# Matrix units and the constant part given other rows in each quarter of an involution and ternary convolution block

## The chip, the core and the metric

The kernel runs on one core of a Trainium2 chip. The metric is the device time of one execution in microseconds (us). The kernel before takes 2158.66 us, the median of 3 runs (2156.32 to 2168.02).

On the core, five engines run side by side, each in the order of its own instructions: TensorE (PE in the profile, its weight loads PEld), VectorE (DVE), ScalarE (ACT), GpSimd (POOL) and SyncE (SP), which issues most of the DMAs. An instruction waits on semaphores for what it needs from other engines.

## What is computed

The input `x` is 8 images of 256 channels, 56 x 56 pixels. Two layers follow each other. The first is an involution: at every pixel and for each of 16 groups of 16 channels a 7 x 7 kernel is made from the normalized input (256 to 64 to 16 x 49 numbers), and the pixel's surroundings are summed with it. The second normalizes, and runs two 3 x 3 convolutions with weights quantized to -1, 0 and 1, each with a batch norm.

```python
# layer 0
ker = einsum('bchw,oc->bohw', gn(x), w_reduce) + b_reduce
ker = (einsum('bchw,oc->bohw', ker, w_span) + b_span).reshape(B, 16, 1, 49, H, W)
patches = ...                                # 7x7 surroundings of gn(x), 16 groups of 16 channels
x = x + (ker * patches).sum(axis=3).reshape(B, C, H, W)
# layer 1
y1 = relu(batch_norm(tri_conv(gn(x), w1)))
x = x + relu(y1 + batch_norm(tri_conv(y1, w2)))
```

`gn` is a group norm of 32 groups. Its scale and shift in layer 0 are not applied to the data: the scale goes into weights and into the outgoing scaling, and the shift times the sum of a pixel's kernel is a "constant part" that is added by itself.

## The kernel before

**Phases.** A first phase does the involution for all images and stores the result, `x1`, to DRAM. Beside it, VectorE finds the quantizing thresholds of the two convolution weights and quantizes them in pieces, a piece at a time (`quantize`, lines 283 to 334; its VectorE work comes four rows apart, in two steps). Then come the two convolutions (`conv_phase`), and a last elementwise pass. The change concerns the first phase only.

**Quarters and rows.** An image is worked off in four quarters `c` of 64 channels (4 groups each). Both halves of the image's height lie side by side on the 128 partitions. A quarter is worked off in ten rows `ty`; rows 0 to 8 stand for three rows of pixels, row 9 for one. `r = c * 10 + ty` counts an image's 40 rows. The main loop (from line 986) goes through the 32 quarters, and in each through the ten rows.

**What a row does**, in the order of the text:

- `store_x1` of the last quarter (rows 2 and 3) or `load_x` of the next image (some rows): DMAs on SP.
- `apply_row` (line 852): TensorE multiplies the pixels' surroundings `q` with the kernel matrices `a` into a PSUM tile `pa` (two of them).
- `prefetch`: the DMA of a `q` for a row five rows ahead, on SP.
- steps of `norm`, which makes the next image's parameters from row 20 on; statistics of the next image and of the finished rows (`gn1_stats`, `gn2_stats`), on VectorE. In row 1, `gn2_stats` takes the last rows of the quarter before.
- `pick_out`: ScalarE (line 862) and VectorE (864) scale the right group of `pa` into `inv`, and GpSimd (868) adds it to `x`.
- `surround`: GpSimd fills the rim of a loaded `q`, three rows ahead (line 751), ScalarE its lower end in two rows of a quarter (764). `rim_of` in row 1 makes the fills for the next quarter (739, 742).
- some steps of `gen`, as many as a table says: this is what the change touches.
- in some rows, a strip: `reduce` makes a part of the next image's 64 reduced features `kr` (TensorE 713, ScalarE 722). Nine strips make an image's features.
- a step of `quant`, the quantizing of the convolution weights, on VectorE.

**The generator.** `generate` makes the next quarter's matrices in 14 units. `UNITS` lists them as (pair of groups, first column, number of columns): six units of 3, 3, 2, 3, 3 and 2 columns, which also have a narrow edge part (`rest`), then eight of 4 columns. Each unit takes a pair of PSUM banks (there are three pairs, `ps_p`, shared with strips and the constant part), TensorE fills it (line 820), ScalarE takes one group out of it (824) and VectorE the other (828). After the units come the two steps of `constant`: TensorE (786) multiplies the features with sums of weights, ScalarE applies the shift (794), and GpSimd adds it to the next quarter's `x` (800), in four operations for the two steps. So a quarter has 16 steps in all, and what is left over is run after row 9.

`PER_ROW` says how many steps of `gen` each row takes; it is one list for every quarter:

```python
PER_ROW = (2, 2, 2, 1, 2, 2, 1, 2, 2, 0)
```

The units are thus at 2, 2, 2, 1, 2, 2, 1, 2 in rows 0 to 7, and the two steps of the constant part in row 8. Below, u0 to u13 are a quarter's units in their order.

**The order.** `pin` ties each engine's instructions to the order of the text, row by row, so what stands above is the order on every engine.

Of the kernel before, what the change touches and what calls it, by code (L numbers as in the profile page):

```python
# [52 lines left out]
         for gp in range(GP) for p0, n in part]  # L53


STRIPS = {24: (0, 0, 3), 26: (0, 3, 3), 27: (0, 6, 4),
          28: (1, 0, 3), 29: (1, 3, 3), 31: (1, 6, 3),
          32: (2, 0, 3), 33: (2, 3, 3), 34: (2, 6, 3)}
A_COLS = (NT * NP + NE * PX) * GQ

PER_ROW = (2, 2, 2, 1, 2, 2, 1, 2, 2, 0)
NQB = 5
PLEAD = 2
RIM_AT = 1
# [25 lines left out]
def involution_tri_block_kernel(  # L90
# [488 lines left out]
    with ExitStack() as ph1:  # L579
# [25 lines left out]
        def load_x(b, c, j):  # L605

            if j == 0:
                xs[b, c] = xpool.tile([P, NHW], F32, tag="x", name=f"x_{b}_{c}")
            part = slice(j * NHW // 2, (j + 1) * NHW // 2)
            nc.sync.dma_start(xs[b, c][:, part], x[b, c, :, part])  # L610
# [47 lines left out]
        def gn2_params(b0, b1):  # L658

            yield from group_norm_params(  # L660
                mv2[:, b0:b1].rearrange("p b t s -> p (b t) s"),
                gn2h[:, b0:b1].rearrange("p b t s -> p (b t) s"), ps_one, f"gn2_{b0}")

            for h in range(2):
                rows = slice(h * CH, (h + 1) * CH)
                nc.vector.tensor_copy(gn2[rows, b0:b1], gn2h[rows, b0:b1, h::2, :])
# [38 lines left out]
        def reduce(b, py, i0, m):  # L705

            ps = ps_pair(f"pk_{b}_{py}_{i0}")
            r0 = i0 * PY + py
            for c in range(NCQ):
                for h in range(2):  # L710
                    rows = slice(h * CH, (h + 1) * CH)
                    src = xs[b, c].rearrange("p (r w) -> p r w", w=W)
                    nc.tensor.matmul(ps[h][:, :m * W], wrn[rows, c, :],  # L713
                                     src[rows, r0:r0 + (m - 1) * PY + 1:PY, :],
                                     start=(c == 0), stop=(c == NCQ - 1))
            whole = min(m, TY - 1 - i0)
            for h in range(2):
                src = ps[h][:, :m * W].rearrange("p (k x) -> p x k", x=PX)
                for n0, k0, k1 in ((h * NT // 2 + i0 * TX, 0, whole * TX),
                                   (NT + h * TX, whole * TX, m * TX)):  # L720
                    if k0 < k1:
                        nc.scalar.activation(kr[py][:, :, n0:n0 + k1 - k0], src[:, :, k0:k1],
                                             AF.Identity, bias=brn)
# [79 lines left out]
        def generate(b, c, a):  # L803

            whole, rest = (v.rearrange("q t (g p) -> q g p t", g=GQ) for v in views(a))
            for u, (gp, p0, n) in enumerate(UNITS):
                ps = ps_pair(f"pg_{b}_{c}_{u}")
                nt = NT + (NE if p0 < PX else 0)  # L810
                g = 2 * gp
                parts = [(whole, 0, NT)] + ([(rest, NT, nt)] if NT < nt else [])

                for j in range(n):
                    py, px = (p0 + j) // PX, (p0 + j) % PX
                    o = py * QX + px
                    for i in range(2):
                        rows = slice(i * CR, (i + 1) * CR)
                        dst = ps[0][:NQ, j:n * nt:n] if i == 0 else ps[1][:NQ, j * nt:(j + 1) * nt]
                        nc.tensor.matmul(dst, wl[rows, c, gp, o:o + NQ], kr[py][rows, px, :],  # L820
                                         start=True, stop=True)
                for j in range(n):
                    for dst, t0, t1 in parts:
                        nc.scalar.activation(  # L824
                            dst[:, g + 1, p0 + j], ps[1][:NQ, j * nt + t0:j * nt + t1],
                            AF.Identity, bias=bt[:, c, g + 1, p0 + j:p0 + j + 1])
                for dst, t0, t1 in parts:
                    nc.vector.tensor_tensor(  # L828
                        dst[:, g, p0:p0 + n].rearrange("q p t -> q t p"),
                        ps[0][:NQ, t0 * n:t1 * n].rearrange("q (t p) -> q t p", p=n),  # L830
                        bt[:, c, g, p0:p0 + n].unsqueeze(1).to_broadcast([NQ, t1 - t0, n]), ALU.add)
                yield
            yield from constant(b, c)

        def apply_row(b, c, a, ty):


            ps = ps_a.tile([P, 512], F32, tag="pa", name=f"pa_{b}_{c}_{ty}")
            row_ps[:] = [ps]
            q = loads.pop((b, c, ty))  # L840
            whole, rest = views(a)
            if ty < TY - 1:
                av, n, t0, t1 = whole, NP, ty * TX, (TY - 1 + ty) * TX
            else:
                av, n, t0, t1 = rest, PX, 0, TX
            m = 32 if ty < TY - 1 else CH
            w = n * m * GQ // CH
            for k in range(TX):
                for h, t in enumerate((t0, t1)):
                    for g in range(CH // m):  # L850
                        o = h * CH + g * m
                        nc.tensor.matmul(ps[o:o + m, k * w:(k + 1) * w], q[:NQ, k, o:o + m],  # L852
                                         av[:, t + k, g * w:(g + 1) * w], start=True, stop=True)
            return ps, n, w // n
# [19 lines left out]
        def prefetch():  # L874
            if queue:
                k = queue.pop(0)
                loads[k] = load_q(*k)
                bare.append(k)
# [9 lines left out]
        def store_x1(b, c, h):  # L888
            nc.sync.dma_start(
                x1_d[b][c // 2][c % 2 * CH:(c % 2 + 1) * CH, h * NHW:(h + 1) * NHW],  # L890
                xs[b, c][h * CH:(h + 1) * CH])
# [3 lines left out]
        def gn2_stats(b, c, ty):  # L895

            if ty == 1:
                gst[b, c] = (small.tile([P, NCB, 6], F32, tag="gn_st2", name=f"st2_{b}_{c}"), 0)
            st, j = gst[b, c]
            while j < NCB and ((j + 1) * NC <= ty * PY * W or ty == TY):  # L900
                image_stats(st, xs[b, c], j)
                j += 1
            gst[b, c] = (st, j)
            if ty == TY:
                nc.vector.bn_aggr(mv2[:, b, c, :], st.rearrange("p n s -> p (n s)"))
# [25 lines left out]
        def matrices(m):  # L931
            return (apool if m % 2 == 0 else apool1).tile(
                [P, A_COLS], F32, tag=f"a{m % 2}", name=f"a_{m}")
# [22 lines left out]

        for i, strip in enumerate(STRIPS.values()):
            reduce(0, *strip)
# [27 lines left out]
        for m, (b, c) in enumerate(quarters):  # L986
            a = a_next
            gen = iter(())
            if m + 1 < len(quarters):
                a_next = matrices(m + 1)  # L990
                gen = generate(*quarters[m + 1], a_next)
            more = b + 1 < B
            for ty in range(TY):
                r = c * TY + ty

                if last is not None and ty in (2, 3):
                    store_x1(*last, ty - 2)
                elif more and r in X_AT:
                    load_x(b + 1, X_AT.index(r) // 2, X_AT.index(r) % 2)
                row = apply_row(b, c, a, ty)  # L1000
                prefetch()

                if r == PARAMS_AT:
                    norm = params(b + 1) if more else gn2_params(0, b)
                next(norm, None)

                if ty == 1 and last is not None:
                    gn2_stats(*last, TY)
                elif ty >= 2:
                    gn2_stats(b, c, ty - 1)  # L1010
                if more and 4 <= r < 20:
                    gn1_stats(b + 1, (r - 4) // NCB, (r - 4) % NCB)
                pick_out(b, c, ty, *row)
                surround()
                if ty == RIM_AT and m + 1 < len(quarters):
                    rim_of(*quarters[m + 1])
                next(norm, None)
                for _ in range(PER_ROW[ty]):
                    next(gen, None)
                if more and r in STRIPS:  # L1020
                    reduce(b + 1, *STRIPS[r])
                if m * TY + ty >= QUANT_AT:
                    next(quant, None)
                pin()
            for _ in gen:
                pass
            last = b, c
# [162 lines left out]
```

## Time and profile before

| what | value |
|---|---|
| median of 3 runs | 2158.66 us |
| profiled execution | 2164.76 us |
| its span, first to last instruction | 2163.0 us |
| mean granted TensorE clock | 0.911 |
| first phase's rows, first apply to last | 62 to 1049 us |
| kernel matrices on TensorE (line 820) | 6144 matmuls, 466.1 us |
| apply on TensorE (line 852) | 17024 matmuls, 290.4 us |
| matrices taken out by ScalarE (824), by VectorE (828) | 530.1 us, 280.9 us |
| constant's adds on GpSimd (800) | 127.2 us, 1024 ns each |
| fill of the rims on GpSimd (751, largest form) | 225.5 us, 705 ns each |

In the lists, a line names a source line, an engine and an operation with what it writes and reads; then come the number of executions, busy time, and the mean of one. A wait `A <- B` is idle time of A that ended when B was done; "issue" is idle time that no semaphore of the profile explains. Durations of neighbours overlap, since engines begin an instruction before the one ahead of it has left. The profiled execution's time is 1.8 us above its span.

### The profile page before, as it was taken

How to read it: one execution, taken by the hardware profiler on the slowest of the kernel's cores; microseconds unless marked ns; L12 is line 12 of the kernel's file. 1: busy time of each engine (PE TensorE's matmuls, PEld its weight loads, DVE VectorE, ACT ScalarE, POOL GpSimd, SP SyncE). 2: the span in 40 equal slices, each digit the busy share in tenths (PEclk: the TensorE clock that was granted, in tenths of full speed). 3: DMA queues.
4: the chain of work that ended last, by engine and by line, in shares of the span. 5: the costliest groups of instructions: out<-in, count | busy, mean ns of one | idle time of the engine just before them, and what ended most of it. 6: DMA issues, size and time to landing. Idle time of an engine off the chain costs nothing.

```text
span 2163.0 us, 70724 instructions
## 1 busy us (share of the span) xinstructions
PE 1759.3 (81%) x29680; PEld 1632.6 (75%) x29680; DVE 1753.4 (81%) x3337; ACT 1432.2 (66%) x3553; POOL 590.7 (27%) x965
## 2 busy tenths in 40 slices
PE   4988988989899898988699999997999999960000
PEld 4777777878777687777699999997999999960000
DVE  5777978787777868877699999998999999984444
ACT  3877787877767677777366666665566666653344
POOL 0555566555546646666200000000000000000000
PEclk9999999999989999999799999998999999985555
DMA  5667777686767758667733333335323333369999
GB/s 184 212 178 232 220 211 236 195 266 197 244 185 218 239 164 263 191 203 201 254 122 122 122 122 122 122 122 189 118 114 124 124 128 128 124 262 425 429 428 397
DMA packets 156250, 440.06 MB, mean 203 GB/s; under 512 B 63774, under 2 KB 74012, under 8 KB 148508
## 3 DMA queue, kind: packets, MB, share of 16 engines
q1 hardware_dynamic: 150336, 405.50, 55.2%
q10 hardware_dynamic: 5596, 30.03, 3.3%
q8 instruction: 235, 3.85, 0.8%
q14 instruction: 83, 0.68, 0.1%
HBM read 323.28 MB, written 112.20 MB: 201 GB/s over the span
## 4 chain that ended last, share of the span: by engine, by line
PE 68%; DMA 10%; DVE 9%; issue 6%; POOL 3%; ACT 3%; ACTq 0%; SPq 0%; POOLq 0%; DVEq 0%
PE c L522 40%; PE pg L820 14%; PE pa L852 8%; PE pk L713 3%; DMA y1f<-y1d 3%; DMA x1f<-x1d 2%; PE ks L786 2%; DMA out_y<-x1f 2%; POOL q L751 1%; DVE x1f L1102 1%; DVE inv L864 1%; ACT a L824 1%; DMA y2f<-y2d 1%; POOL x L868 1%; DMA q<-in_x_nb 1%
## 5 line engine op out<-in xcount | busy, mean ns | idle before, releaser
L522 PE MATMUL c<-pl,wq 128*128 128x392 f32 x4608 | 857.7, 348 | 14.9 <-ACT pl L392 14.9
L522 PEld LDWEIGHTS c<-pl,wq 128*128 128x128 f32 x4608 | 855.7, 190 | 16.7 <-ACT pl L392 15.3
L824 ACT ACTIVATE a<-pg,bt 126x126 f32<-126x126 f32 (+1 forms) x2048 | 530.1, 469 | 110.1 <-PE pg L820 109.5
L820 PE MATMUL pg<-kr,wl 64*126 64x140 f32 (+1 forms) x6144 | 466.1, 296 | 41.2 <-issue 16.4
L820 PEld LDWEIGHTS pg<-kr,wl 64*126 64x126 f32 x6144 | 405.5, 198 | 67.2 <-issue 24.3
L852 PE MATMUL pa<-a,q 126*32 126x48 f32 x17024 | 290.4, 215 | 67.0 <-issue 52.6
L852 PEld LDWEIGHTS pa<-a,q 126*32 126x32 f32 x17024 | 242.1, 116 | 135.4 <-issue 83.6
L828 DVE TENSOR_TENSOR a<-pg,bt 126x504 f32<-126x504 f32 (+4 forms) x640 | 280.9, 480 | 54.4 <-PE pg L820 52.8
L868 POOL TENSOR_TENSOR x<-x,inv 128x168 f32<-128x168 f32 x320 | 167.0, 522 | 404.1 <-DVE inv L864 370.7
L864 DVE SCALAR_TENSOR_TENSOR inv<-pa,gn1s,inv 128x168 f32<-128x168 f32 (+1 forms) x384 | 134.2, 351 | 154.6 <-ACT inv L862 151.1
L392 ACT CAST pl<-r 128x812 fp32r<-128x812 f32 x192 | 162.5, 868 | 143.4 <-DVE r L387 122.8
L372 POOL MEMSET xp<- 128x116 f32 x32 | 6.3, 196 | 826.1 <-DVE a L387 826.1
L751 POOL TENSOR_TENSOR q<-q,sides 126x256 f32<-126x256 f32 (+1 forms) x320 | 225.5, 705 | 3.1 <-DMA q<-in_x_nb 3.1
L393 DVE TENSOR_TENSOR pl<-r,pl 128x812 fp32r<-128x812 f32 x192 | 186.6, 998 | 27.6 <-ACT pl L392 26.3
L457 ACT ACTIVATE dummy<-y,nc 128x1568 f32<-128x1568 f32 (+1 forms) x128 | 200.2, 1564 | 4.8 <-DVE y L542 3.5
L862 ACT ACTIVATE inv<-pa,gn1s 128x168 f32<-128x168 f32 x320 | 134.9, 423 | 69.5 <-PE pa L852 49.3
L149 DVE BATCH_NORM_STATS2 st<-x 128x6 f32<-128x392 f32 x256 | 137.8, 554 | 16.4 <-DMA x<-in_x 10.1
L800 POOL TENSOR_TENSOR x<-x,add 128x504 f32<-128x504 f32 (+1 forms) x128 | 127.2, 1024 | 25.4 <-ACT add L794 25.4
L1049 ACT ACTIVATE xp<-raw,gn 128x392 f32<-128x392 f32 (+1 forms) x124 | 82.5, 721 | 61.3 <-DVE a L387 61.0
L1069 ACT ACTIVATE xp<-raw,bi_bn,sc_bn 128x392 f32<-128x392 f32 (+1 forms) x124 | 82.3, 720 | 58.8 <-DVE a L387 57.1
L1100 DVE SCALAR_TENSOR_TENSOR y1f<-y2f,sc_bn,y1f 128x3136 f32<-128x3136 f32 (+2 forms) x20 | 56.6, 2831 | 64.6 <-DMA y2f<-y2d 50.6
L713 PE MATMUL pk<-x,wrn 64*128 64x168 f32 (+1 forms) x1152 | 101.0, 316 | 0.0
(174 smaller groups left out, 1789.2 us busy)
## 6 DMA issues: line engine op xcount, KB each, us to landing
q<-in_x_nb SPq DMA_DIRECT2D x320, 448.0 KB, 4.2
raw<-x1d SPq DMA_DIRECT2D x32, 812.0 KB, 5.9
raw<-y1d SPq DMA_DIRECT2D x32, 812.0 KB, 6.1
x<-in_x SPq DMA_DIRECT2D x64, 392.0 KB, 5.3
x1d<-x SPq DMA_DIRECT2D x64, 392.0 KB, 5.2
y1d<-y SPq DMA_DIRECT2D x30, 784.0 KB, 3.7
y2d<-y SPq DMA_DIRECT2D x30, 784.0 KB, 3.4
y1f<-y1d SPq DMA_DIRECT2D x14, 1568.0 KB, 14.4
```

Source lines behind the costliest of these rows:

```text
L392: nc.scalar.copy(hi, r)
L393: nc.vector.tensor_tensor(lo, r, hi.bitcast(F32), ALU.subtract)
L457: nc.scalar.activation(dst, v, f, bias=shift[:, to:to + 1], accum_out=stats[:, to, j, n:n + 1])
L522: nc.tensor.matmul(ps[:, to, :NM], wq[k][:, t, dx, to * P:(to + 1) * P], part[:, t, :, dx:dx + W], start=(c == 0), stop=(c == last))
L713: nc.tensor.matmul(ps[h][:, :m * W], wrn[rows, c, :], src[rows, r0:r0 + (m - 1) * PY + 1:PY, :], start=(c == 0), stop=(c == NCQ - 1))
L751: nc.gpsimd.tensor_tensor(v, v, z, ALU.add)
L820: nc.tensor.matmul(dst, wl[rows, c, gp, o:o + NQ], kr[py][rows, px, :], start=True, stop=True)
L824: nc.scalar.activation(dst[:, g + 1, p0 + j], ps[1][:NQ, j * nt + t0:j * nt + t1], AF.Identity, bias=bt[:, c, g + 1, p0 + j:p0 + j + 1])
L828: nc.vector.tensor_tensor(dst[:, g, p0:p0 + n].rearrange("q p t -> q t p"), ps[0][:NQ, t0 * n:t1 * n].rearrange("q (t p) -> q t p", p=n), ...
L852: nc.tensor.matmul(ps[o:o + m, k * w:(k + 1) * w], q[:NQ, k, o:o + m], av[:, t + k, g * w:(g + 1) * w], start=True, stop=True)
L864: nc.vector.scalar_tensor_tensor(iv, parts[:, :, g], scale[:, g:g + 1], iv, ALU.mult, ALU.add)
L868: nc.gpsimd.tensor_tensor(xv, xv, iv.rearrange("p t (y x) -> p y t x", x=PX), ALU.add)
```

## The change

The list of steps becomes a list for each of the four quarters, and the first strip goes from row 24 to row 25.

```diff
-STRIPS = {24: (0, 0, 3), 26: (0, 3, 3), 27: (0, 6, 4),
+STRIPS = {25: (0, 0, 3), 26: (0, 3, 3), 27: (0, 6, 4),
           28: (1, 0, 3), 29: (1, 3, 3), 31: (1, 6, 3),
           32: (2, 0, 3), 33: (2, 3, 3), 34: (2, 6, 3)}
...
-PER_ROW = (2, 2, 2, 1, 2, 2, 1, 2, 2, 0)
+PER_ROW = ((2, 2, 1, 2, 1, 2, 1, 2, 1, 2), (2, 2, 1, 2, 1, 2, 1, 2, 1, 2),
+           (2, 2, 2, 2, 2, 1, 1, 1, 1, 2), (2, 1, 1, 1, 1, 2, 2, 2, 2, 2))
...
-                for _ in range(PER_ROW[ty]):
+                for _ in range(PER_ROW[c][ty]):
                     next(gen, None)
                 if more and r in STRIPS:
                     reduce(b + 1, *STRIPS[r])
```

Each new list adds up to 16 as well. The strips are in rows 5 to 9 of quarter 2 (before: 4, 6, 7, 8, 9) and in rows 1 to 4 of quarter 3. A row with a strip takes one unit, but for row 9 of quarter 2, which has a strip and the constant part. In quarters 0 and 1 the rows take two units and one by turns from row 1 on. The constant part's two steps come in row 9 of each quarter.

## The prediction

> **What bounds the kernel now.** I read the page first (engine shares, slices, the chain of waits), then the windows of one image by quarter, then the list of waits, then the timeline around one quarter boundary.
>
> ```profile
> span 2163.0 us, 70724 instructions
> PE 1759.3 (81%) x29680; PEld 1632.6 (75%) x29680; DVE 1753.4 (81%) x3337; ACT 1432.2 (66%) x3553; POOL 590.7 (27%) x965
> PE   4988988989899898988699999997999999960000
> POOL 0555566555546646666200000000000000000000
> PE c L522 40%; PE pg L820 14%; PE pa L852 8%; PE pk L713 3%; DMA y1f<-y1d 3%; DMA x1f<-x1d 2%; PE ks L786 2%; DMA out_y<-x1f 2%; POOL q L751 1%; DVE x1f L1102 1%; DVE inv L864 1%; ACT a L824 1%; DMA y2f<-y2d 1%; POOL x L868 1%; DMA q<-in_x_nb 1%
> ```
>
> POOL is busy in the first 20 slices of 54 us only: that is the first phase, 62 us (first apply of a row) to 1049 us, and the only one that the change touches. The convolutions after it and the final pass stay. In the first phase PE is at 8 to 9 tenths, and all four engines are well loaded. The windows of the fourth image, one line per quarter (columns: length, then busy PE, PEld, DVE, ACT, POOL, granted clock, DMA share):
>
> ```profile
> 430.87:461.78 30.91, 23.29 (x744) 19.61 (x741) 26.29 (x69) 23.28 (x83) 17.02 (x29) 1.00 0.83 275
> 461.78:490.42 28.64, 24.94 (x741) 21.18 (x741) 25.31 (x69) 21.46 (x78) 19.30 (x31) 0.94 0.80 238
> 490.42:527.61 37.19, 34.90 (x852) 30.25 (x849) 26.05 (x74) 26.96 (x95) 21.45 (x33) 0.91 0.55 178
> 527.61:555.99 28.38, 27.41 (x806) 23.76 (x804) 19.58 (x47) 24.46 (x88) 15.33 (x28) 1.00 0.69 213
> ```
>
> The reader is to see two kinds of quarters. In the fourth (strips in rows 1 to 4) PE is busy 27.4 of 28.4 us: no order of units can give much. In the first two PE idles, 7.6 and 3.7 us, and DVE is busier than PE. I took the start of every apply row from the timeline: over the first seven images the quarters last 30, 29, 38 and 28 us, while the shortest execution of each row, added up, gives 21.8, 22.7, 31.8 and 26.6. So some 22 us an image are lost, nearly all in quarters 0, 1 and rows 0 to 4 of quarter 2. What ends PE's waits from 60 to 1050 us (columns: us in total, times, longest):
>
> ```profile
> PE pa L852 <- issue: 52.6, 49, 3.2
> ACT sq_a L137 <- DVE ve_a L135: 17.3, 7, 4.0
> PE pg L820 <- issue: 16.4, 11, 4.3
> PE pg L820 <- ACT a L824: 13.2, 12, 2.4
> PE pg L820 <- DVE a L828: 10.4, 10, 2.0
> PE pa L852 <- POOL q L751: 9.4, 6, 5.1
> ```
>
> The largest, "issue", about 69 us, ends no semaphore: it falls in the middle of an apply row too, and counted along PE's stream nearly all such stalls over 0.3 us begin multiples of 256 instructions apart. The clock drops to half in 23 stretches, 137 us together, nearly each behind a gap of 1 to 3 us, so a gap costs more than itself.
>
> The boundary before the fourth image, POOL, DVE and PE lines:
>
> ```profile
> 430.95 4.00 POOL L800 TENSOR_TENSOR x<-x,add 128x504 f32<-128x504 f32 x4
> 434.91 0.30 POOL L868 TENSOR_TENSOR x<-x,inv 128x56 f32<-128x56 f32 x1
> 435.18 0.72 POOL L751 TENSOR_TENSOR q<-q,sides 126x256 f32<-126x256 f32 x1
> 433.47 1.29 DVE L317 TENSOR_TENSOR piece_w<-piece_w 128x48 f32<-128x48 f32 x1
> 434.68 0.34 DVE L318 TENSOR_TENSOR piece_w<-piece_w 128x48 f32<-128x48 f32 x1
> 436.97 0.60 PE L820 MATMUL pg<-kr,wl 64*126 64x140 f32 x5 [1.61 <-DVE a L828]
> ```
>
> The constant's adds hold POOL for 4.00 us. The last row's own add and the fill of the next quarter's row 2 stand behind them, the weight pieces on DVE are stretched by them (0.20 us elsewhere for the L317 form), and PE waits 1.61 us for the unit that DVE gets to late.
>
> **What the Trainium skill says.** "SBUF — State Buffer", § "SBUF: two separate sides": DVE and GpSimd share one port pair as an exclusive lock, held for a whole instruction, against DVE operations with two SBUF inputs. The trace agrees: 1.29 us instead of 0.20. "TensorE: Matmul & The Clock Gate", Part 1: the clock goes to half after an idle window of about 3.4 us. The trace shows half clock in multiples of 3.4 us, but behind shorter gaps (1.5 to 2.5 us). "Runtime: NRT & Kernel Launch", § "Instruction fetch mechanics": instructions come in blocks of 256 by a DMA queue of the sequencer's own, mostly hidden. The stalls at multiples of 256 fit the block, not the word "hidden".
>
> **The change part by part.** No instruction is added or removed: every quarter still runs 14 units and 2 constant steps, every image 9 strips. The moved steps issue no DMA, so SP's queue keeps its order; they pass other work on PE, ScalarE, DVE and POOL alone. PE's work is unchanged, about 103 us an image by the shortest rows; only waits and slow clock can move.
>
> *Constant from row 8 to row 9.* Before, rows 8 and 9 take 2.59 and 0.94 us at full clock; with a unit (0.92) in row 8 and the constant's matmuls (2.59 - 0.85 for a lone apply = 1.7) in row 9 they take about 1.8 and 2.6. POOL's adds still begin about when row 0 of the next quarter begins (430.95 against 430.87 here; they follow the constant's ScalarE adds, which start within a microsecond of its matmuls). But POOL now has, ahead of them, row 9's add (0.30) and the fill for row 2 (0.72); behind them row 0's add (0.54) and the fill for row 3 (0.73). Old slack: adds end at +2.8 to +4.0, the fill at +3.9 to +5.0, row 2 due at +2.36 + 2.12 = 4.5. New: the fill at +5.1 to +6.3, row 3 due at 4.5 + 1.6 = 6.1 (row 2 has one unit in quarters 0 and 1). That is some 0.4 us better. PE's waits for the fill at a row 2 were 0.86, 1.64, 0.70 and 0.62: 3.8 us; I take 3 us off.
>
> *Weight pieces of a row 9.* They follow row 9's picking on DVE. Row 9 is longer by 1.7 us and the adds begin at its end instead of its start, so the five operations run in about 1 us instead of the 3 here. That should remove the PE waits on DVE of 1.90 (189 us), 1.61 (437) and 2.00 (721), 5.5 us, and two stretches of half clock of 3.4 us, worth 1.7 each. I take 7 off these 8.9. The last rows' statistics in row 1, which waited 0.89 us on DVE behind row 9's add at 591, also come free: under 1 us.
>
> *Quarter 2.* In images 0 to 2 the parameter matmul at row 2.0 waits 1.3 to 2.5 us for DVE's statistics, which the longer row 9 would shorten. It gains nothing: the square root on ScalarE, which waits for DVE's chain up to 4.03 us, holds units up next. Rows 0 to 4 took 21.3, 22.1 and 19.5 us in the images with the wait, and 20.8, 23.3, 23.1, 20.3 in those without. I take zero. Rows 0 to 2 are as before (2, 2, 2), row 3 gets a second unit while ScalarE is still late (two units and a pick, 2.5 us, against PE's 3.3 with the parameter matmuls), row 4 loses its strip. Cover: three pairs of PSUM banks, two units of lead. Cost 0 to 0.5 us an image, taken 1 us in all. Rows 5 to 9 have ScalarE at 13 us against PE's 16, so no wait; they already ran without gaps.
>
> *Quarter 3* is PE-bound before and after: zero. *Strips:* only the first moves, row 24 to 25, away from the parameters' last step: zero to 0.3 us an image, taken as zero.
>
> *Quarters 0 and 1, single units spread.* ScalarE's unit costs 1.3 us for three columns with the edge, 1.03 for four, 0.88 for two (from runs of 12, 8 and 10 operations), PE's 0.75, 0.92, 0.50. Rows 0 to 2 want 3.0 + 2.6 + 2.6 of ScalarE against 6.6 of PE; with u5 moved to row 3 the peak of its lag falls by some 0.3 us. On the other side the constant's two pairs are now taken right ahead of row 0, where the third is all that is free: 0 to 0.7 us per boundary, taken 1.5 us in all, the rest being the rival below. Strips and pieces that follow row 0 and 1 meet the adds as before: plus 1.
>
> *Fetch.* The shortest stretches of 128 matmul pairs by the row times: 20% under 3.3 us before, 18% after. Taken as zero, with 5 us either way.
>
> Sum: -3 - 7 - 0.5 + 1 + 1.5 + 1 = about -7 us. The profiled execution took 2164.8 us (span 2163.0), so about 2157.5 under the profiler; against the median shown, 2158.7, this is 2151.5. I say 2151.
>
> **Rivals.** *Cascade:* the waits feed each other, through the half clock and through ScalarE behind DVE. Half of the named dependency waits of PE (13.2 + 10.4 + 9.4 of the list, and 5.3 at row 2.0: 38) would go, 19 us, and with them some 9 us of slow stretches: 2131. For it: 137 us at half clock follow such gaps. Against: half of these sit behind fetch stalls or the square root. *Slower:* the constant's two PSUM pairs. At row 0, the second unit may start only when ScalarE has drained the first constant pair, about 1.3 us after it is filled if ScalarE is on time; PE reaches that unit 2.45 us after. If ScalarE is more than 1.1 us late at row 9 this binds, in a place where the old order had an empty row; behind the waiting matmul stand all of PE's later rows, and the reading of these by ScalarE and DVE. At 0.7 us each over 31 boundaries: +22 us, 2181. For it: ScalarE needs about 22 us a quarter, as PE does. *Reshuffle:* the loss is set by fetch and square root, and nothing moves: 2157.
>
> **How the numbers follow.** Forecast (0 to -15 us) 0.46; cascade 0.21; slower 0.21; reshuffle 0.12. 0.5% is 10.8 us, about what a measurement here can tell from no change. A third of the forecast's chance and nearly all the cascade's lie beyond it: faster 0.37. Slower 0.20, the same 0.43. Range: down to the cascade's middle, up to most of the slower case, 2132 to 2174; the forecast's own is 2144 to 2159.
>
> **What would show it.** Right: POOL's 0.30 add of row 9 and the next fill stand ahead of the four adds; pieces' operations after row 9 near 0.2 us; PE's waits on DVE under 6 us and on the fill under 7; the square root's 17 us and the issue's 69 as before. Wrong: new PE waits on ScalarE in rows 0 and 1 (slower), or a total of half clock under 110 us (cascade).

## The result and the profile after

| | before | after |
|---|---|---|
| median of 20 runs each, us | 2161.54 | 2163.97 |
| profiled execution, us | 2164.76 | 2159.04 |
| its span, us | 2163.0 | 2157.3 |
| mean granted TensorE clock | 0.911 | 0.917 |

The ratio of the times is 1.0005, with a 95% interval of 0.9988 to 1.0021. The change makes no difference that can be told. The forecast of -7 us would be 0.9968 and lies outside the interval.

The two profiled executions differ by 5.7 us in the change's favour, but they are a lucky pair: the one before lies 3 us above its kernel's median, the one after 5 us below its own, and the 20 runs of the changed kernel spread from 2152.7 to 2173.1 us. Their clocks mislead in the same way. Over the 136 executions of the kernel before that ran beside the experiments below the mean granted clock was 0.9154, and over the 20 of the changed kernel 0.9146. So one execution can't decide a question of 7 us. In what follows the traces tell where waits went, and repeated runs tell what that was worth.

The page of the kernel after:

```profile
span 2157.3 us, 70705 instructions
PE 1748.1 (81%) x29680; PEld 1619.6 (75%) x29680; DVE 1751.9 (81%) x3337; ACT 1436.7 (67%) x3553; POOL 588.1 (27%) x965
```

The busy time of every engine is the same within 13 us. The first phase, from its first apply row to the end of its last, takes 982.2 us, and took 985.6; the rest is the same within 2.3 us. The fourth image by quarter (columns: length, then busy PE, PEld, DVE, ACT, POOL, granted clock, DMA share, GB/s):

```profile
434.13:465.29 31.16, 23.15 (x743) 19.56 (x741) 25.33 (x69) 21.93 (x82) 18.01 (x29) 1.00 0.83 268
465.29:493.75 28.46, 24.52 (x743) 20.93 (x741) 25.57 (x68) 22.09 (x82) 18.27 (x30) 0.94 0.83 247
493.75:531.62 37.87, 34.53 (x851) 29.98 (x849) 26.09 (x71) 28.05 (x96) 19.80 (x32) 0.91 0.57 177
531.62:560.90 29.28, 27.61 (x806) 23.72 (x804) 20.26 (x49) 23.99 (x90) 16.45 (x28) 1.00 0.66 206
```

No quarter is more than 1 us away from its length before, and PE still idles 8.0 and 3.9 us in the first two. But the reasons of the idling are others. What ends waits from 60 to 1050 us (us in total, times, longest):

```profile
PE pa L853 <- issue: 70.4, 66, 3.0
...
ACT sq_a L138 <- DVE ve_a L136: 18.3, 7, 3.3
...
PE pg L821 <- issue: 13.2, 12, 3.0
PE pg L821 <- ACT a L825: 12.1, 12, 1.8
...
PE pa L169 <- DVE d_a L166: 10.9, 7, 2.6
...
PE pa L853 <- POOL q L752: 6.1, 2, 5.7
...
PE pg L821 <- DVE a L829: 1.9, 3, 1.0
```

(The lines of the source are one further on than before.) The wait for a unit's VectorE part fell from 10.4 to 1.9 us, the wait for a fill from 9.4 to 6.1, all of it at the phase's end. Two grew: "issue" from 69.0 to 83.6, and one that was 1.2 us before, a matmul of the parameters (L169) that waits for VectorE's square of differences (L166), to 10.9. All of PE's gaps in the phase's rows, added up along the trace, were 117.2 us and are 123.4. The time at half clock was 136.5 and is 109.2 us, but by the clocks of the many runs above that difference belongs to these two executions and not to the change.

The boundary before the fourth image, lines of POOL, DVE and PE, to be read beside the boundary in the prediction. Row 0 begins at 434.13:

```profile
434.25 0.32 POOL L869 TENSOR_TENSOR x<-x,inv 128x56 f32<-128x56 f32 x1 [2.62 <-PE ks L787]
434.53 0.72 POOL L752 TENSOR_TENSOR q<-q,sides 126x256 f32<-126x256 f32 x1
435.21 3.95 POOL L801 TENSOR_TENSOR x<-x,add 128x504 f32<-128x504 f32 x4
434.20 0.20 DVE L318 TENSOR_TENSOR piece_w<-piece_w 128x48 f32<-128x48 f32 x1
...
435.24 1.29 DVE L321 SCALAR_TENSOR_TENSOR piece_w<-piece_w 128x48 f32<-128x48 f32 x1
...
437.23 1.46 PE L821 MATMUL pg<-kr,wl 64*126 64x140 f32 x20
```

Row 9's own add and the next fill now stand ahead of the four adds of the constant part, three of the five weight operations run at 0.2 to 0.3 us (the fourth takes 0.76, and the last, beside the adds, 1.29), and PE goes on with row 1's units with no wait for VectorE. That is the order that the prediction described. The adds, however, begin 1.1 us after row 0 (before: 0.1), because row 9's add, ahead of them on POOL, waits for VectorE's picking of row 9, and that comes at 433.3 to 434.2. At the boundary ahead of quarter 2, counted from its row 0 and averaged over the eight images, the adds began at +0.62 and ended at +4.59 us, and now begin at +1.52 and end at +5.45.

Row 2.1 of the second image shows what these late adds meet (POOL, DVE, PE lines of the kernel after):

```profile
246.03 3.92 POOL L801 TENSOR_TENSOR x<-x,add 128x504 f32<-128x504 f32 x4
...
247.77 0.75 DVE L165 TENSOR_TENSOR d_a<-mv,gm_a 128x4 f32<-128x4 f32 x1
248.55 1.17 DVE L166 TENSOR_TENSOR d_a<-d_a 128x4 f32<-128x4 f32 x1
...
249.77 0.39 PE L169 MATMUL pa<-d_a,grp_sb 128*128 128x4 f32 x2 [2.61 <-DVE d_a L166]
```

Two operations on four elements a partition take 0.75 and 1.17 us beside the adds, and PE stands 2.61 us for the second of them, with row 2.1's units behind it. The square itself was stretched before, too (columns: shortest, median and longest, in ns):

```profile
L165 DVE TENSOR_TENSOR d_a<-d_a x7: 403/1178/1187, 121.5 to 875.4; 128x4 f32<-128x4 f32 x7
```

In the first three images it took 0.40 us, since the wait for the statistics at row 2.0 held the chain until the adds were over; in the other four it took 1.18. Now that this wait is gone, the chain meets the adds in all seven images, and its first operation is stretched as well (a median of 0.21 us before, 0.89 after). One wait has thus taken the other's place: rows 0 and 1 of quarter 2 together take a mean of 7.5 us before and after.

The other new loss is "issue". Such a stall in the middle of an apply row, PE's lines of the kernel after:

```profile
191.20 0.80 PE L853 MATMUL pa<-a,q 126*32 126x48 f32 x55
194.94 0.24 PE L853 MATMUL pa<-a,q 126*32 126x48 f32 x1 [2.95 <-issue]
```

A row's 56 matmuls stop after 55 for 2.95 us, with nothing that the last of them waits for. The DMA part of the page has a queue for PE's instructions:

```profile
q8 instruction: 235, 3.85, 0.7%
```

It moved 235 packets, 3.85 MB: 16 KB each, one for 256 PE instructions. The stall above ends 1.5 us after such a packet, which was on its way from 192.53 to 193.43 us. Of the issue stalls over 1 us, 28 of 29 before and 31 of 35 after end 1.2 to 1.65 us after the end of one. In the first phase a packet sets out a median of 1.5 us after PE has passed the block boundary before it (0.2 to 3.5 for nine in ten), so PE has about one block in hand: 101 of 193 blocks before and 100 after are entered within 1.7 us of their landing. In the convolutions the packets land 22 to 29 us ahead, which is also about one block, since they follow each other there by about 24 us. "Runtime: NRT & Kernel Launch", § "Instruction fetch mechanics", of the Trainium skill has the block of 256 right; its "mostly hidden" doesn't hold for this phase, with 69 and 84 us of stalls.

### The profile page after: what moved, and what is told of

Same layout as the page of the kernel before. It is cut to its first block, busy times and chain, and to the rows that moved or that the text cites. A ratio compares the mean times of both kernels' runs of the same rounds, so it can differ in the third digit from the quotient of the medians.

```text
span 2157.3 us, 70705 instructions
## 1 busy us (share of the span) xinstructions
PE 1748.1 (81%) x29680; PEld 1619.6 (75%) x29680; DVE 1751.9 (81%) x3337; ACT 1436.7 (67%) x3553; POOL 588.1 (27%) x965
## 3 DMA queue, kind: packets, MB, share of 16 engines
q8 instruction: 235, 3.85, 0.7%
## 4 chain that ended last, share of the span: by engine, by line
PE 69%; DMA 10%; issue 7%; DVE 6%; POOL 5%; ACT 3%; SPq 0%; ACTq 0%; POOLq 0%; DVEq 0%
PE c L523 40%; PE pg L821 15%; PE pa L853 9%; DMA x1f<-x1d 4%; PE pk L714 3%; DMA y1f<-y1d 3%; POOL q L752 2%; DMA out_y<-x1f 2%; POOL x L869 2%; PE ks L787 1%; ACT a L825 1%; DVE x1f L1103 1%; POOL x L801 1%; DVE a L829 1%; DMA sums<-in_w_all 1%
## 5 line engine op out<-in xcount | busy, mean ns | idle before, releaser
L825 ACT ACTIVATE a<-pg,bt 126x126 f32<-126x126 f32 (+1 forms) x2048 | 537.4, 474 | 95.5 <-PE pg L821 94.0
L821 PE MATMUL pg<-kr,wl 64*126 64x140 f32 (+1 forms) x6144 | 464.8, 295 | 27.7 <-issue 13.2
L863 ACT ACTIVATE inv<-pa,gn1s 128x168 f32<-128x168 f32 x320 | 135.5, 424 | 72.7 <-PE pa L853 53.8
L150 DVE BATCH_NORM_STATS2 st<-x 128x6 f32<-128x392 f32 x256 | 137.8, 554 | 10.4 <-DMA x<-in_x 9.4
L801 POOL TENSOR_TENSOR x<-x,add 128x504 f32<-128x504 f32 (+1 forms) x128 | 126.3, 1017 | 24.1 <-ACT add L795 24.1
```

The source lines that it names most:

```text
L801: nc.gpsimd.tensor_tensor(x_, x_, v, ALU.add)
L825: nc.scalar.activation(dst[:, g + 1, p0 + j], ps[1][:NQ, j * nt + t0:j * nt + t1], AF.Identity, bias=bt[:, c, g + 1, p0 + j:p0 + j + 1])
```

## The experiments

The theory: in quarters 0 and 1, PE is paced by the arrival of its instructions, whose packets come late where the DMAs move much data; a wait on a semaphore that is taken away there comes back as an issue stall (fetch). The rival: the gain is lost at row 2.1, where the later adds stretch VectorE's chain, which then holds the square root and quarter 2 (chain). Ratios are to the kernel before, run on the same chip, with 95% intervals. A gap's sum by quarter is over the first seven images, from PE's stream.

**Half of each load of `q`.** Both kernels with only the first half of each `q` row loaded, into five fixed tiles that were zeroed once; the involution is thus computed from stale columns, and the time is that of the same instructions with 224 KB instead of 448 KB for each load.

```diff
-            q = qpool.tile([P, TX, P], F32, tag="q", name=f"q_{b}_{c}_{ty}")
-            nc.sync.dma_start(q.rearrange("p k c -> p (k c)"),
-                              x_nb[b, c, (HQ - QY - PY * ty) * QX:(HQ - QY - PY * ty) * QX + P, :])
+            q = qfix[len(loaded_q) % NQB]
+            loaded_q.append(1)
+            n = TX * P // 2
+            nc.sync.dma_start(q.rearrange("p k c -> p (k c)")[:, :n],
+                              x_nb[b, c, (HQ - QY - PY * ty) * QX:(HQ - QY - PY * ty) * QX + P, :n])
```

> The kernel before, but of each q only the first half of its columns is loaded, 224 KB instead of 448; the rest stays as it was set to zero at the start, and every engine's work is kept. Theory (TensorE's instruction blocks come late because of the data DMAs, and quarters 0 and 1 run at that pace): PE's issue waits of 69 us fall below 35, half clock falls too, and the kernel is 30 to 60 us faster, about 2115. Rival (the issue waits are something else, or the engines' dependencies take over): issue waits stay above 55 us, and the time stays within 10 us of the kernel before.

> The changed kernel with the same halved loads. Theory (the waits that the change took away were given to the instruction blocks): with the blocks in time the change shows its gain, so this is 5 to 15 us faster than the halved kernel before, about 2105. Rival (the new wait for the parameter chain at row 2.1 is what eats the gain): this equals the halved kernel before within 4 us.

Before with halved loads: 0.9886 (0.9858 to 0.9914), after: 0.9835 (0.9807 to 0.9863). The medians, 2133.64 and 2123.62, are 10 us apart; from the six runs of each, the difference of the means lies between about 3 and 16 us (an estimate). Waits of the first, then of the second (60 to 1050 us):

```profile
PE pa L854 <- issue: 22.9, 36, 3.5
...
PE pg L822 <- issue: 12.4, 17, 1.9
```

```profile
PE pa L855 <- issue: 45.7, 49, 2.6
...
PE pg L823 <- issue: 6.2, 9, 1.4
```

With half the bytes, issue stalls fall from 69 to 35 us and from 84 to 52, and the two kernels are 28 and 38 us below the kernel before (30 to 60 was expected of the first). So the loads' traffic is a cause of the stalls. The change's own gain, nothing with full loads, is about 10 us with half of them. The chain doesn't explain that, since PE's wait at row 2.1 is still 9.3 us there.

But the exchange doesn't vanish: the changed kernel still has 17 us more of issue, and the gaps add up to the same (96.6 and 97.1 us). Its gain goes with the clock: 105.8 and 88.7 us at half clock in the two traces, and a mean granted clock of 0.916 and 0.921 over the six runs of each, where with full loads the clock didn't rise. So it is shown that the data's traffic keeps the change from paying; that the added stalls alone do so is not shown.

**Only some of the lists.** New lists in quarters 0 and 1 alone (`only01`, first strip at 24), in quarters 2 and 3 alone (`only23`, first strip at 25), and the change without its list for quarter 1 (`q1_old`).

```diff
# only01
+PER_ROW = (N01, N01, OLD, OLD)
# only23
+PER_ROW = (OLD, OLD, (2, 2, 2, 2, 2, 1, 1, 1, 1, 2), (2, 1, 1, 1, 1, 2, 2, 2, 2, 2))
# q1_old
+PER_ROW = (N01, OLD, (2, 2, 2, 2, 2, 1, 1, 1, 1, 2), (2, 1, 1, 1, 1, 2, 2, 2, 2, 2))
# N01 = (2, 2, 1, 2, 1, 2, 1, 2, 1, 2), OLD = (2, 2, 2, 1, 2, 2, 1, 2, 2, 0)
```

> The new lists in quarters 0 and 1 alone; quarters 2 and 3 and the first strip as before. Theory (quarters 0 and 1 hold all that the change moves: waits on DVE and fills go, instruction blocks and the parameter chain take it back): PE's waits on VectorE's units under 4 us, L169 near 11 us, issue waits 80 us or more, time within 6 us of the kernel before. Rival (the new lists of quarters 2 and 3 are what costs): 10 us or more faster than the kernel before.

> The old list in quarters 0 and 1, the new ones and the moved strip in quarters 2 and 3. Theory: these two quarters are paced by TensorE before and after, so issue waits stay near 70 us, VectorE's waits near 10, and the time within 5 us of the kernel before. Rival (one unit beside a strip helps or harms): 8 us or more away from it.

> The changed kernel with the old list in quarter 1 alone. Theory (in the change, GpSimd's adds of the constant stand behind row 9's own add, which waits for DVE, so they begin later and lie across the parameter chain of quarter 2): PE's wait at L169 falls from 11 us to under 3, and PE's wait for the statistics at L157 returns with 3 to 6 us; time within 6 us of the changed kernel. Rival (the chain is late for another reason): L169 stays above 8 us.

Measured: `only01` 1.0039 (1.0019 to 1.0058), slower; `only23` 0.9975 (0.9960 to 0.9990), faster; `q1_old` 0.9967 (0.9951 to 0.9983), faster. The first and the third lie further away than the 6 us that were expected. The two halves add up to the whole: 1.0039 x 0.9975 = 1.0014, within the interval of the change. The change thus holds a gain of about 5 us from the lists of quarters 2 and 3, and a loss of about 8 us from those of quarters 0 and 1; taking back one list of ten numbers gains about 8 us on the changed kernel (by the two intervals, 3 to 13). Waits of `q1_old`:

```profile
PE pa L853 <- issue: 63.2, 60, 2.7
...
PE pg L821 <- issue: 9.5, 9, 3.9
...
PE pa L169 <- DVE d_a L166: 4.9, 5, 1.2
```

With the old list in quarter 1 the wait at row 2.1 is 4.9 us (under 3 was expected), and issue is 72.7; in `only01` they are 12.2 and 79.4. Where the time is lost isn't the same in each trace, though. In `only01` it is quarter 0 that is longer, 31.5 us against 29.8, and quarter 1 that is shorter, 28.8 against 29.3; in `q1_old` it is quarter 1 that is shorter than in the changed kernel, 28.0 against 29.4. So these two times 8 us need not be one and the same loss.

**Quarter 1's list taken apart.** Old spread of units with the constant part in row 9 (`q1_const9`), and new spread with it in row 8 (`q1_const8`); the other quarters as changed.

```diff
# q1_const9, quarter 1
-           (2, 2, 1, 2, 1, 2, 1, 2, 1, 2),
+           (2, 2, 2, 1, 2, 2, 1, 2, 0, 2),
# q1_const8, quarter 1
-           (2, 2, 1, 2, 1, 2, 1, 2, 1, 2),
+           (2, 2, 1, 2, 1, 2, 2, 2, 2, 0),
```

> The changed kernel, but quarter 1 has the old spread of its units and only its constant moved, from row 8 to row 9. Theory (in quarter 1 it is the constant's place that costs: the adds end a microsecond later across the parameter chain): L169 waits 8 us or more, time like the changed kernel's, 2158 to 2166. Rival (the spread of single units is what costs): L169 under 6 us, and the time near 2155.

> The changed kernel, but quarter 1 keeps its constant in row 8 while its units are spread as in the change up to row 5 (two units in rows 6 to 8, the constant's steps in place of a row's units in row 8). Theory: L169 under 6 us, time 2151 to 2158. Rival (the spread costs): 2160 or more.

Measured: 0.9999 (0.9983 to 1.0015) and 0.9987 (0.9962 to 1.0012). The wait at row 2.1 follows the constant part's place, 11.1 us with row 9 and 5.3 with row 8, but the times don't tell which half carries the 8 us: neither alone gives the 0.9967 of `q1_old` clearly, and their intervals overlap. The issue stalls, in turn, follow the spread of the units. Over all the traces with full loads (those of the experiments below too), in us over seven images:

```
                                             issue stalls   waits on semaphores
quarter 1, old spread of units  (6 traces)   17.7 to 25.8   9.0 to 13.2
quarter 1, new spread           (9 traces)   25.7 to 33.3   1.2 to  4.9
quarter 3, old list             (4 traces)    5.6 to  8.7   0.0 to  0.6
quarter 3, new list            (11 traces)    8.7 to 15.5   0.0 to  0.8
```

In quarter 1 one is exchanged for the other at about one to one (a mean of 21.4 against 29.2 for issue, 11.2 against 2.7 for semaphores), as the theory of fetch has it. In quarter 0 the pair of before and after shows no exchange (issue 30 and 31 us, semaphores 6 and 0), and the means over four and eleven traces do (26 against 30, 5 against 2). In quarter 3 there is nothing to exchange, and issue grows nonetheless: a quarter 3 lasted 28.0 to 28.8 us with the old list, 28.8 to 29.8 with the new. Why the new order of units and strips meets its blocks worse there stays open.

**Without the adds of the constant part.** The changed kernel, with GpSimd's adds (L801) left out; the output lacks the constant part.

```diff
-                    nc.gpsimd.tensor_tensor(x_, x_, v, ALU.add)
```

> The changed kernel without the constant's adds on GpSimd (126 us of GpSimd work left out; all else kept). Theory (these adds hold VectorE's small operations through the shared port): L169 under 3 us, VectorE's d*d under 0.3 us instead of 1.2, waits for fills only in the last quarter, and still no large gain, since the blocks of instructions pace quarters 0 and 1: issue waits 85 us or more, time 2140 to 2155. Rival (the adds are the bound of these quarters): issue waits as before and the time under 2130.

0.9940 (0.9915 to 0.9965), some 14 us less than the changed kernel with its adds: that is what the adds cost the others in all. The square of differences and PE's wait for it, without the adds:

```profile
L166 DVE TENSOR_TENSOR d_a<-d_a x8: 163/648/655, 25.9 to 857.1; 128x4 f32<-128x4 f32 x8
```

```profile
PE pa L169 <- DVE d_a L166: 2.9, 5, 0.9
```

Its median goes from 1166 to 648 ns (under 300 was expected), and PE's wait from 10.9 to 2.9 us. So it is the adds that stretch VectorE at row 2.1. "SBUF — State Buffer", § "SBUF: two separate sides", of the Trainium skill describes an exclusive lock between GpSimd and VectorE operations with two inputs in SBUF; these two are such, and the runs agree as far as the stretch goes, 1.17 us beside the adds and 0.65 without them.

**The square root a row later.** In the changed kernel, ScalarE's square root of the parameters, which waits for VectorE's chain, is put behind a row's work.

```diff
         nc.vector.tensor_scalar(ve, var, eps, None, ALU.add)
+        yield
         sq = small.tile([P, n], F32, tag=f"rs_sq{n}", name=f"sq_{name}")
...
-        rs = rstd_of(var, GN_EPS, name)
+        rs = yield from rstd_of(var, GN_EPS, name)
...
-            for _ in range(3):
+            for _ in range(2):
                 yield
```

> The changed kernel with the parameters' square root, and what follows it, one step later, so that ScalarE meets it in row 2.2 when its input is long there. Theory (quarter 2 is not paced by instruction blocks, so waits taken away there count in full): ScalarE's 18 us at the square root go to under 3, PE's 12 us on ScalarE at row 2.2 to under 3, half clock falls by 20 us or more, and the time by 12 to 25 us, about 2145. Rival (the lost time in quarter 2 comes from DVE's chain itself and returns at the next wait): within 6 us of the changed kernel, 2160.

0.9957 (0.9942 to 0.9971), 9 us faster than before and 10 faster than the changed kernel, where 12 to 25 was expected. Waits:

```profile
PE pa L170 <- DVE d_a L167: 8.4, 5, 2.7
...
PE pg L827 <- DVE a L835: 8.2, 9, 2.1
...
ACT sq_a L139 <- DVE ve_a L136: 4.4, 4, 2.0
```

ScalarE's wait of 18.3 us is down to 4.4, and PE waits for ScalarE's half of a unit no more (12.1 before); some of it comes back as a wait for VectorE's half, 8.2. So a wait that is taken away in quarter 2 is worth time; in the changed kernel this quarter has 1.4 us of issue stalls, against 31 and 33 in quarters 0 and 1.

**The whole parameter chain a row later.** `PARAMS_AT` from 20 to 21: alone (`params21`), with the square root's edit (`params21_sqrt`), and the latter with the old list, first strip at 25 (`old_params21_sqrt`).

```diff
-        PARAMS_AT = 20
+        PARAMS_AT = 21
```

> The changed kernel with the parameter chain a row later, from row 21 on, which the moved strip leaves room for. Theory (the chain's small VectorE operations in row 2.0 are held by the constant's adds on GpSimd; a row later the adds are over): PE's 11 us at L169 fall under 3, and the time by 5 to 12 us against the changed kernel, about 2153. Rival (the wait follows the chain): L169 stays above 8 us, and the time at 2160 or more.

> Both: the chain from row 21 on, and its square root a step later. Theory: the two gains are in quarter 2, which instruction blocks don't pace, so they add: L169 under 3 us, ScalarE at the square root under 4 us, rows 0 to 4 of quarter 2 under 18.5 us (21.1 in the changed kernel), and 20 to 30 us faster than the kernel before, about 2137. Rival: the second removes little once the first is gone, 2148 or more.

> The lists of the kernel before with the first strip at row 25, the chain from row 21 and the late root. Theory (what the lists save is taken back by instruction blocks and the chain; with the chain out of the way only the blocks are left): 2143 to 2155, 0 to 8 us slower than the changed lists with the same chain (2144). Rival (the new lists are the worse ones, and the chain was all the gain): 2138 or less.

0.9927 (0.9906 to 0.9949), 0.9915 (0.9889 to 0.9940) and 0.9921 (0.9895 to 0.9946). All are faster than both kernels, by some 16 to 18 us; their intervals overlap. Rows 0 to 4 of quarter 2 take 17.4, 17.1 and 17.4 us instead of 21.1 after and 21.5 before. The wait at row 2.1 was expected to go with it, to under 3 us. It doesn't; the second's waits:

```profile
PE pa L859 <- issue: 68.8, 66, 4.0
...
PE pg L827 <- issue: 13.4, 12, 2.4
PE pa L170 <- DVE d_a L167: 11.7, 7, 3.3
```

What went is the square root's hold: in `params21` it waits 8.7 us instead of 18.3, and PE's wait for ScalarE's half of a unit is 1.2 instead of 12.1. Half clock is down to 78.5 us in the trace of `params21_sqrt`, and the mean clock of its six runs is 0.921, where the kernel before has 0.915 on the same chip. So a wait of this size for the square of differences doesn't keep a kernel from being 16 us faster; what the wait itself is worth, this doesn't tell. And with the square root's hold out of the way, new lists and old list can't be told apart.

**The second matmul of the chain moved.** With the square root's edit, the parameters' second matmul goes behind row 2.1's picking (`spaced`), or ahead of row 2.2's (`spaced2`); `old_spaced2` is the latter with the old list.

```diff
# spaced
         nc.vector.tensor_tensor(d, d, d, ALU.mult)
         yield
+        yield
# spaced2
-        yield
+        for _ in range(3):
+            yield
         ps2 = psum_tile(f"gnp2_{name}")
```

> The changed kernel with the parameter chain from row 20 on, but its second matmul behind row 1's picking and its variance and square root in row 2.2, so that each step's input is ready when its engine meets it. Theory: L169 under 3 us, ScalarE at the square root under 4 us, rows 0 to 4 of quarter 2 under 18 us, 2135 to 2145, no slower than the version with the chain from row 21. Rival (a new wait takes the place): L169 or ScalarE above 8 us, 2150 or more.

> The changed kernel with the parameter chain spread: first matmul and differences in row 2.0, second matmul ahead of row 2.2's picking, variance behind it, square root in row 2.3, bias in row 2.4. Theory (quarter 2 is not paced by instruction blocks, so its waits count in full): waits at the second matmul under 2 us (11.7 in the version with the chain from row 21 and a late root), rows 0 to 4 of quarter 2 at 15.5 to 16.5 us, time 2130 to 2142, 5 us or so faster than that version. Rival (DVE itself is late there, and the wait goes to the units): waits on VectorE's units or parameters in quarter 2 above 8 us, 2144 or more.

> The lists of the kernel before with the first strip at row 25 and the spread chain. Theory: 2136 to 2150, within 8 us above the changed lists with the spread chain. Rival (new lists are worse): 4 us or more below these.

`spaced` is slower than before, 1.0049 (1.0035 to 1.0064), where 2135 to 2145 us was expected, against 2158 for the kernel before on that chip. `spaced2` gives 0.9933 (0.9907 to 0.9959), no faster than `params21_sqrt`, and `old_spaced2` 0.9928 (0.9901 to 0.9954). One line of the waits of `spaced`, then two of `spaced2`:

```profile
PE pa L171 <- DVE inv L872: 36.0, 8, 4.9
```

```profile
PE pa L860 <- issue: 58.9, 57, 3.5
...
PE pg L828 <- DVE a L836: 17.1, 16, 2.7
```

In `spaced` the matmul (L171) writes spare columns of the row's own PSUM tile, which VectorE still reads for the picking, and PE stands 4.5 us a time. In `spaced2` the wait at row 2.1 is gone, and waits for VectorE's half of the units stand in its place, 17.1 us: VectorE itself is late in those rows, and a matmul that no longer waits for it only hands the wait on.

## Why the prediction was wrong

The failing step is **Fetch**: "The shortest stretches of 128 matmul pairs by the row times: 20% under 3.3 us before, 18% after. Taken as zero, with 5 us either way." Issue stalls went from 69.0 to 83.6 us, 15 us more, in the pair of traces; over all the traces, new lists go with 4, 8 and 4 us more in quarters 0, 1 and 3. The working asked whether PE would be faster between block boundaries, and not what PE does when a wait is taken away in a stretch that is paced by its instructions: it arrives at the next block as much earlier, and the block is not there. The measure of 3.3 us was also too small. In the trace before, a packet sets out a median of 1.5 us after the last boundary, takes 1.0, and PE goes on some 1.4 after its end: about 3.9 us a block (an estimate from these three medians), and 101 of 193 blocks were entered within 1.7 us of their landing, half and not a fifth. The sum thus added waits as though each were time of its own. In quarter 1 they were exchanged one to one. That the issue stalls are fetch and stand at the blocks was read rightly from the trace; the price of it was missing from every term of quarters 0 and 1. That stalls took the place of waits is shown; that they alone took the 7 us isn't, since with halved loads they grew as much and the change did pay, by the clock.

**Constant from row 8 to row 9.** The order came as foretold, row 9's add and the fill ahead of the adds, and the fills cost nothing any more at a row 2 (3.8 us gone; -3 was taken). Wrong was "POOL's adds still begin about when row 0 of the next quarter begins": they begin 0.7 to 2.3 us later than they did, 1.0 ahead of quarters 1 and 2, since the row's own add that was put ahead of them depends on VectorE. Ahead of quarter 2 they then meet the parameters' chain, and the wait at row 2.1 grew by 9.7 us. The prediction had this chain on its list, but only as a wait that would shrink and gain nothing ("the parameter matmul at row 2.0": that wait did go, from 5.3 us to none). As rows 0 and 1 of quarter 2 last 7.5 us either way, the grown wait isn't a loss against the kernel before. With the constant part's place alone put back in quarter 1 the ratio is 0.9987, without it 1.0005, with overlapping intervals.

One effect of the place doesn't show in the times. The constant part of quarter 3 is made during quarter 2 from `kr`, which the next image's strips overwrite meanwhile: before, those of rows 24, 26 and 27 come ahead of the constant's row 28; after, those of rows 25 to 28 ahead of row 29. For this quarter both kernels thus take features of the next image in part, for all images but the last, and the changed kernel takes one strip more of them.

**Weight pieces of a row 9** (-7): right as to the waits, 10.4 to 1.9 us where 5.5 was named. Not borne out as to the clock, which was to give 3.4 of the 8.9 us: half clock fell by 27 us in the pair of traces, but the mean clock of the many runs is 0.9154 before and 0.9146 after. Rows 0 and 1 of a quarter 0 and 1 became 1.5 us shorter, 6.20 to 4.64 and 7.00 to 5.51. Most of the time was given back later in the same quarters, which last 29.0 and 29.4 us where they lasted 29.8 and 29.3.

**Quarter 2** (zero): rows 0 to 4 take 21.1 us against 21.5, and the square root kept its wait (18.3 against 17.3) and set them, as was said; `after_sqrt` shows that it is worth about 9 us. **Quarter 3** (zero) cost: a mean of 29.2 us against 28.0, some 8 us over seven images and the largest loss of the pair, with issue stalls 5.6 to 11.4. "PE-bound" was read as safe. That a busy PE crosses block boundaries fastest fits this, and no run tests it. That the lists of quarters 2 and 3 together still gain 0.25% in `only23` comes with shorter rows 0 and 1 of the quarters that follow them (4.67 instead of 6.20 us in quarter 0).

**The rivals.** *Slower*, by the constant's two PSUM pairs, didn't come: PE's wait for ScalarE's units is 12.1 us against 13.2. *Cascade's* sign, under 110 us at half clock, came true at 109.2 by the luck of the execution that was traced: the clocks of all the runs show no such fall. *Reshuffle*, "the loss is set by fetch and square root, and nothing moves", gave 2157 and was nearest in its mechanism: it had 0.12. What spoke for it stood on the page, 69 us of issue as the largest wait, twice the 33 us of PE's waits for units and fills together. What wasn't weighed is where those 69 us lie: 48 of the 59 in the seven images are in quarters 0 and 1, where the 7 us of the weight pieces were to be gained (189, 437 and 721 us).

Still open: which part of quarter 1's list carries its 8 us; why quarter 3 meets its blocks worse; and why the change raises the clock with halved loads and not with full ones.

## What to carry to other kernels

Before waits are added up to a gain, ask for each what would hold the engine next if it were gone, and take the idle time that no semaphore explains as such a holder: look whether it begins multiples of a fixed number of instructions apart and ends just after a packet of the instruction queue, and in which stretches. In such stretches, fewer bytes of data were worth more here than a better order, 28 us against none; fewer instructions were not tried. In a stretch without such stalls (here quarter 2) a wait taken away from the square root was worth 10 us. An operation that is put behind another on an in-order engine takes over all that the other waits for, which should be followed to the next place where it stretches a neighbour's work. And before a trace's clock is credited to a change, hold it against the clocks of the other runs: here one pair of traces showed a fall in half clock that 156 runs don't.

## What the hardware showed that was not expected

- PE's instruction packets set out only 1.5 us (median) after PE had passed the block boundary before, where the data DMAs were busy at a share of 0.72, and in 59 of 64 stalls over 1 us PE went on 1.2 to 1.65 us after a packet's end. Halving the largest loads (share 0.55) took away 32 to 34 us of stalls.
- An operation on 128x4 elements took 1.17 us beside GpSimd's adds, 0.65 in the same place without them, and 0.16 at the shortest: for these small operations on VectorE the neighbour was most of the price.
- A matmul into unused columns of a PSUM tile waited for a reader of other columns of it: 36 us in 8 times. The wait is on a semaphore of the program; that the memory itself would need it is not shown.
